# One core, cross attention: the first activations on one queue, normalised before the transpose, and later loads at other slots

## The chip, the cores and the metric

The kernel runs on one core of one Trainium2 chip. The metric is the device time of one execution in microseconds (us). The engines are named as the profile names them: PE is the matrix engine (PEld its weight loads), DVE the vector engine, ACT the scalar engine, POOL the general-purpose engine, and SP the engine that issues nearly all DMAs here. An engine works through its own instructions in order; it waits for another only on a semaphore.

## The reference

```python
x = (hidden_states - mu) * jax.lax.rsqrt(var + LN_EPS) * ln_gamma + ln_beta
Q = _split_heads(x @ Wq.T)
K = _split_heads(memory_keys)          # memory_keys and memory_values are the same ctx
V = _split_heads(memory_values)
scores = jnp.einsum('bhsd,bhtd->bhst', Q, K) * scale
scores = jnp.where(attention_mask[:, None, None, :], scores, -jnp.inf)
probs = jax.nn.softmax(scores, axis=-1)
attn = jnp.einsum('bhst,bhtd->bhsd', probs, V)
out = attn.transpose(0, 2, 1, 3).reshape(B, S, HIDDEN) @ Wout.T
return residual + out
```

There are 8 batches of 256 query rows and 256 context rows, 1024 columns, 32 heads of 32, all in float32. The mask has a batch's 256 context positions.

## The kernel before

**Slots.** The work is cut into 64 slots: slot `n` belongs to batch `n // 8` and to four heads. In each slot PE makes the scores of the next slot (`sc`), the product of probabilities and values of the slot two before (`pv`), and pieces of the query projection (`pq`, weights `wq`) and the output projection (`po`, weights `wo`). DVE adds the mask and finds the extreme of each row (`e`, `mn`), ACT takes the exponentials, POOL (and in places ACT and DVE) divides by the sum, DVE transposes blocks of 32 into `pT`, ACT puts half of that aside in `pc`, and two pairs of DMAs (`pT<-pT`, then `pT<-pc`) bring the blocks to the partitions where `pv` reads them.

**Batches.** Batches 0 and 1 take plain projections. From batch 2 on (`SPLIT = 2`) the query projection is made of seven half-size products with sums and differences of weights, and the same is done for the output projection. The derived query weights `T1` and `T3` don't fit beside the others: they are built once in a buffer called `ring`, stored to memory (`kept_T`), and loaded back into `ring` for each later batch in the order T1, B11, T3. The derived output weights are made on POOL by `sum_wo` from the loaded blocks `B11`, `B12`, `B21`, `B22`, each loaded in two pairs of chunks by `load_wo`.

**Order.** Nothing reorders the work: each engine's instructions stand as the code emits them. The tables `loads`, `stats`, `norms`, `trans`, `moves`, `rings` say at which slot a batch's `x` is loaded, normalised, transposed, and moved, and at which slot `ring` is refilled. What stands in the list `between` of a slot is issued on SP between that softmax's `pT<-pT` and its `pT<-pc`; the first eight softmaxes do this one slot later than the others. Eight DMA semaphores go round, so a DMA also waits for the eighth one before it.

**The start.** `x[0]` is loaded in two row blocks `s` = 0 and 1, 128 rows each. Block 0 comes in two column halves, one issued by SP and one by ACT; block 1 comes whole. PE first runs 26 transposes of a constant (`busy`) until data is there. For block 0, DVE subtracts the mean and builds a diagonal matrix of the reciprocal deviations, and PE multiplies each chunk by it: transposing and scaling in one product. Block 1 is normalised whole on DVE and transposed plainly. ACT and DVE copy the eight transposed chunks from `px` to `xnT` with gamma and beta (`copy_x0`), and `first_q` multiplies each chunk with the first query weights as it comes.

```python
x0 = xs[0][:, 0, :]
nc.vector.tensor_scalar(x0, x0, mean, None, ALU.subtract)
diag = ring[:, 0, 1, :]
nc.vector.tensor_scalar(diag, ident, rstds[0][:, 0:1], None, ALU.mult)
ln_stats(0, 1)
transpose_x0(0, diag)
early, late = (0, 1, 2, 3, 6, 7), (4, 5)
for c in early + late:
    copy_x0(0, c, nc.vector if c > 5 else nc.scalar)
ln_norm(0, 1, nc.vector)
first_q(0, early + late)
transpose_x0(1)
```

Of the kernel before, what the change touches and what calls it, by code (L numbers as in the profile page):

```python
# [51 lines left out]
P = 128  # L52
# [7 lines left out]
def xattn_kernel(  # L60
# [54 lines left out]


    busy = ps_s.tile([P, P], F32, tag="sc", name="busy")
    for _ in range(26):
        nc.tensor.transpose(busy, ident, ident)


    xs, ks, vs, rs = {}, {}, {}, {}

    def load_x(b, s, h=None, queue=nc.sync):
# [4 lines left out]
        queue.dma_start(xs[b][:, s, cols], x[b, ts(s, P), cols])  # L129

    def load_k(n):

# [91 lines left out]
    def ln_stats(b, s, parts=range(3), later=None):  # L224


        if s == 0 and 0 in parts:
            mvs[b] = sm.tile([P, NS, 2], F32, tag="mv", name=f"mv_{b}", bufs=2)
            rstds[b] = sm.tile([P, NS], F32, tag="rstd", name=f"rstd_{b}", bufs=2)
        if 0 in parts:  # L230
            sts[b, s] = sm.tile([P, 2, 6], F32, tag="st", name=f"st_{b}_{s}", bufs=2)
        for h in range(2):
            if h in parts:
                nc.vector.bn_stats(sts[b, s][:, h, :], xs[b][:, s, ts(h, 512)])  # L234
        if 2 not in parts:
            return
        nc.vector.bn_aggr(mvs[b][:, s, :], sts[b, s].rearrange("p h k -> p (h k)"))
        ve = sm.tile([P, 1], F32, tag="ve", name=f"ve_{b}_{s}", bufs=2)
        nc.vector.tensor_scalar(ve, mvs[b][:, s, 1:2], LN_EPS, None, ALU.add)

        def pow_():
            nc.gpsimd.tensor_tensor(rstds[b][:, s : s + 1], ve, mhalf[:, :1], ALU.pow)

        if later is None:
            pow_()
        else:
            later.append(pow_)

    def ln_norm(b, s, engine):
        if engine is nc.scalar:  # L250
            shift = sm.tile([P, 1], F32, tag="shift", name=f"shift_{b}_{s}", bufs=2)
            nc.gpsimd.tensor_scalar(
                shift, mvs[b][:, s, 0:1], rstds[b][:, s : s + 1], -1.0, ALU.mult, ALU.mult
            )
            engine.activation(
                xs[b][:, s, :], xs[b][:, s, :], AF.Identity,
                bias=shift, scale=rstds[b][:, s : s + 1],
            )
            return
        engine.tensor_scalar(  # L260
            xs[b][:, s, :], xs[b][:, s, :], mvs[b][:, s, 0:1], rstds[b][:, s : s + 1],
            ALU.subtract, ALU.mult,
        )

# [1 line left out]
    xnTs[0] = lambda c: xnT0[:, c, :]  # L266
    px0 = {}

    def transpose_x0(s, diag=None):

        pool, tag, k = (ps_v, "pv", NC // 2) if diag is None else (ps_s, "sc", 2)
        for g in range(NC // k):
            pt = pool.tile([P, k, P], F32, tag=tag, name=f"px0_{s}_{g}")
            for i in range(k):
                px0[s, k * g + i] = pt[:, i, :]
                chunk = xs[0][:, s, ts(k * g + i, P)]
                if diag is None:
                    nc.tensor.transpose(pt[:, i, :], chunk, ident)
                else:
                    nc.tensor.matmul(pt[:, i, :], chunk, diag, start=True, stop=True)  # L280

    def copy_x0(s, c, engine):

# [523 lines left out]
    for n in range(N):  # L807
# [9 lines left out]
    assert not any(n in products and new_qs[n] for n in range(N))  # L817


    loads, stats, norms, trans, moves, biases, masks = (  # L820
        {n: [] for n in range(N)} for _ in range(7)
    )
    for b in range(1, B):
        first = NQ * (b - 1) + 2
        if b == 1:
            when = dict(moves=())
        elif b == 2:
            when = dict(
                loads=(0, 1), stats=(2, 3), norms=(3, 4), trans=(4, 5),
                moves=tuple(5 + (i + 2) // 6 for i in range(16)),  # L830
            )
        else:
            when = dict(
                loads=(first - 12, first - 11) if b == SPLIT + 1 else (first - 13, first - 12),
                stats=(first - 10, first - 8) if b == SPLIT + 1 else (first - 11, first - 9),
                norms=(first - 8, first - 7), trans=(first - 7, first - 6),
                moves=tuple(first - 6 + (i + 2) // 6 for i in range(16)),
            )
        for table, key in (
            (loads, "loads"), (stats, "stats"), (norms, "norms"), (trans, "trans"),  # L840
        ):
            for i, n in enumerate(when.get(key, ())):
                assert n < first
                table[n].append((b, i))
# [42 lines left out]
    x0 = xs[0][:, 0, :]  # L887
    mean = mvs[0][:, 0, 0:1]
    nc.vector.tensor_scalar(x0, x0, mean, None, ALU.subtract)
    diag = ring[:, 0, 1, :]  # L890
    nc.vector.tensor_scalar(diag, ident, rstds[0][:, 0:1], None, ALU.mult)
# [52 lines left out]
    for n in range(N):  # L944
# [8 lines left out]
        if n + 3 in firsts or n + 2 in firsts:  # L953
            between, ahead = between + ahead, []
        if b >= 0:
            if b == B - 2 and i - 1 in (5, 6):
# [217 lines left out]
```

## Time and profile before

| | before |
|---|---|
| median of three runs | 562.32 us (562.32 to 562.91) |
| the profiled execution | 562.78 us |
| its span in the trace | 560.9 us |
| PE busy | 555.3 us, 99% of the span |
| DVE, ACT, POOL busy | 466.5 us (83%), 423.6 us (76%), 392.9 us (70%) |
| DMA queue of SP | 117.48 MB, 69.9% of sixteen engines' span |
| granted PE clock | full in all forty slices |

The span runs from the first to the last instruction on the core; the profiled execution took 1.88 us more than its span and 0.46 us more than the median run. A row of the timeline gives the start, the length, the engine, the line, what is written from what, the shapes and the count; in square brackets stands how long the engine idled before and who released it. A row with a count over one merges neighbours.

### The profile page before, as it was taken

The numbers are of one execution on the slowest core, as the hardware profiler recorded it, in microseconds if no ns is written. First come the engines' busy times: TensorE is split into PE (matmuls) and PEld (weight loads), VectorE is DVE, ScalarE is ACT, GpSimd is POOL, SyncE is SP. The second block draws the span as 40 slices with busy tenths as digits, with TensorE's granted clock in tenths as the row PEclk, the third lists the DMA queues.
The fourth block names the chain that finished last, engine by engine and source line by source line (L and its number), as shares of the span: only waits on it lengthen the run. The fifth ranks groups of instructions, "written<-read, shape, count | busy, mean of one in ns | idle before, by whom it ended". The sixth has DMA issues, their size and how long they took to land.

```text
span 560.9 us, 24340 instructions
## 1 busy us (share of the span) xinstructions
PE 555.3 (99%) x9334; PEld 356.9 (64%) x9334; DVE 466.5 (83%) x1716; ACT 423.6 (76%) x1464; POOL 392.9 (70%) x635
## 2 busy tenths in 40 slices
PE   8999999999999999999999999999999999999997
PEld 7666665767656767567765676567766766744443
DVE  5979889999998888988898888988888878879823
ACT  3699999998769867797777967778776876769920
POOL 1688887999797566867568566777648657448780
PEclk9999999999999999999999999999999999999999
DMA  8967658966688867887788677788658974536752
GB/s 301 398 189 210 184 152 239 300 191 185 203 291 244 234 186 199 271 226 235 199 244 246 197 194 220 235 236 242 180 157 242 256 214 132 145 95 182 217 161 76
DMA packets 47236, 119.30 MB, mean 213 GB/s; under 512 B 8976, under 2 KB 9744, under 8 KB 47120
## 3 DMA queue, kind: packets, MB, share of 16 engines
q1 hardware_dynamic: 46832, 117.48, 69.9%
q8 instruction: 74, 1.21, 0.9%
q14 instruction: 42, 0.34, 0.2%
q10 hardware_dynamic: 288, 0.27, 0.1%
HBM read 66.33 MB, written 11.53 MB: 139 GB/s over the span
## 4 chain that ended last, share of the span: by engine, by line
PE 97%; DVE 1%; DMA 1%; ACT 0%; POOL 0%; issue 0%; POOLq 0%
PE po_S L216 20%; PE pq_A L216 19%; PE pv L643 12%; PE sc L493 12%; PE po_A L216 11%; PE pq L216 10%; PE pq_S L216 7%; PE po_end L216 3%; PE po_last L216 1%; DMA x<-in_x_dram 1%; PE po_end_s L216 0%; PE px L280 0%; PE px L314 0%; ACT e L535 0%; DVE st L234 0%; DVE xnT L289 0%
## 5 line engine op out<-in xcount | busy, mean ns | idle before, releaser
L550 POOL TENSOR_SCALAR e<-e,rden 128x256 f32<-128x256 f32 x466 | 215.4, 479 | 124.6 <-DVE rden L542 122.1
L535 ACT ACTIVATE e<-e,mn 128x256 f32<-128x256 f32 x512 | 254.1, 502 | 43.3 <-DVE mn L531 42.8
L556 DVE STREAM_TRANSPOSE pT<-e 128x512 f32<-128x512 f32 x256 | 178.9, 703 | 36.6 <-POOL e L550 27.7
L531 DVE CUSTOM_DVE_ANT_0 e<-sc,mb 128x256 f32<-128x256 f32 x512 | 185.3, 416 | 23.5 <-PE sc L493 23.1
L562 ACT COPY pc<-pT 128x512 f32<-128x512 f32 x128 | 78.9, 616 | 53.1 <-DVE pT L556 34.7
L535 ACT ACTIVATION_READ_ACCUMULATOR e<-e,mn 128x1 f32 x512 | 98.4, 192 | 0.0
L493 PEld LDWEIGHTS sc<-k,qa 32*128 32x128 f32 x1024 | 46.1, 184 | 45.7 <-issue 20.8
L643 PE MATMUL pv<-pT,v 64*32 64x128 f32 x4096 | 74.5, 274 | 0.0
L493 PE MATMUL sc<-k,qa 32*128 32x256 f32 x1024 | 73.7, 401 | 0.2 <-ACT qa L301 0.2
L216 PE MATMUL po_S<-wo,at 128*64 128x512 f32 x304 | 73.5, 599 | 0.0
L643 PEld LDWEIGHTS pv<-pT,v 64*32 64x32 f32 x4096 | 57.2, 105 | 22.8 <-issue 10.8
L216 PE MATMUL po_A<-wo,at 128*64 128x512 f32 x256 | 58.6, 599 | 0.0
L216 PE MATMUL pq<-xnT,wq 128*64 128x256 f32 (+3 forms) x544 | 58.4, 369 | 0.0
L216 PEld LDWEIGHTS pq_A<-xnT,wq 128*64 128x64 f32 x832 | 46.3, 137 | 7.4 <-issue 6.3
L216 PE MATMUL po_S<-wo,s 128*64 128x512 f32 x208 | 49.5, 599 | 0.0
L216 PEld LDWEIGHTS pq<-xnT,wq 128*64 128x64 f32 x544 | 36.8, 137 | 18.8 <-issue 1.8
L216 PE MATMUL pq_A<-xnT,wq 128*64 128x128 f32 x832 | 47.6, 273 | 0.0
L542 DVE RECIPROCAL rden<-den 128x2 f32<-128x2 f32 x256 | 38.3, 150 | 5.9 <-ACT e L535 4.9
L531 DVE DVE_READ_ACCUMULATOR2_ANT mn<- 128x1 f32 x512 | 42.5, 83 | 0.0
L216 PEld LDWEIGHTS po_A<-wo,at 128*64 128x64 f32 x256 | 16.9, 137 | 30.0 <-issue 29.1
L216 PEld LDWEIGHTS po_S<-wo,at 128*64 128x64 f32 x304 | 19.3, 137 | 22.6 <-issue 22.6
L656 ACT COPY at<-pv 128x128 f32<-128x128 f32 x128 | 26.1, 253 | 8.7 <-PE pv L643 8.7
(99 smaller groups left out, 645.2 us busy)
## 6 DMA issues: line engine op xcount, KB each, us to landing
v<-in_kv_dram SPq DMA_DIRECT2D x32, 512.0 KB, 4.6
pT<-pT SPq DMA_DIRECT2D x128, 128.0 KB, 2.8
pT<-pc SPq DMA_DIRECT2D x128, 128.0 KB, 4.1
ring<-kept_T SPq DMA_DIRECT2D x20, 512.0 KB, 6.0
k<-in_kv_dram SPq DMA_DIRECT2D x32, 256.0 KB, 4.3
x<-in_x_dram SPq DMA_DIRECT2D x15, 512.0 KB, 6.0
r<-in_x_dram SPq DMA_DIRECT2D x28, 256.0 KB, 5.0
out_dram<-r SPq DMA_DIRECT2D x28, 256.0 KB, 2.8
```

The source lines that it names most:

```text
L216: nc.tensor.matmul(out[ts(w, P // 2)], stationary[:, ts(w, P // 2)], moving, **flags)
L493: nc.tensor.matmul(scs[n][j][:, s, :], qa[r, n % NQ, ts(s, P)], ks[n - n % 2][r, n % 2, :], start=True, stop=True,)
L531: nc.vector.tensor_tensor_reduce(out=e[:, s, :], in0=pss[j][:, s, :], in1=mbs[n // NQ], scale=1.0, scalar=NO_SCORE, op0=ALU.add, op1=ALU.m ...
L535: nc.scalar.activation(e[:, s, :], e[:, s, :], AF.Exp, bias=mn[:, s : s + 1], scale=-1.0, accum_out=den[:, s : s + 1],)
L542: nc.vector.reciprocal(rden, dens[j])
L550: engine.tensor_scalar(es[j][:, s, :], es[j][:, s, :], rden[:, s : s + 1], 1.0, ALU.mult, ALU.mult,)
L556: nc.vector.transpose(pT[:, :, :, j, :, :].rearrange("p a i s k -> p (a i) s k"), es[j].rearrange("p s (b t) -> p b s t", t=K),)
L562: nc.scalar.copy(pc[:, :, ts(j, 2)], pT[:, 1, :, ts(j, 2)])
L643: nc.tensor.matmul(pvs[n][r][j * HD : (j + 1) * HD], vs[n - n % 2][ts(r, 2 * K), i, ds(n % 2 * P + j * HD, HD)], pT[ts(r, 2 * K), :, i, j, ...
L656: nc.scalar.copy(ats[b, k][:, c, :, ts(r, 2), :], pv.rearrange("p a s k -> p s a k"))
```

## The change

The start and four groups of later loads are different; the counts of PE's, POOL's and ACT's instructions after the start, and their order, are the same.

- All of `x[0]` goes on SP, in four halves; ACT issues no load of `x`.
- DVE normalises block 0 in two halves with both operands at once (`ln_norm` gained a parameter `h`), and PE transposes it plainly. The statistics of block 1's first half stand ahead of that, those of its second half behind it.
- ACT copies five of the eight chunks and DVE three (it was six and two), and the products take them in another order. Block 1 is normalised in halves too. `busy` has 25 transposes.
- `x[2]`'s block 0 is loaded in the prologue and its block 1 in slot 0; two loads of output weights move from the prologue to slots 1 and 2, and two from slots 2 and 4 to slots 3 and 5.
- `T1` for batch 3 is loaded into `ring` in slots 14 and 15 (it was 15 and 16); `x[4]` is loaded at the end of slot 12 and in slot 13 (it was 13 and 14).

```diff
-    for _ in range(26):
+    for _ in range(25):
         nc.tensor.transpose(busy, ident, ident)
...
     load_x(0, 0, 0)
-    load_x(0, 0, 1, nc.scalar)
+    load_x(0, 0, 1)
     nc.scalar.activation(gs[:, :NS], mhalf, AF.Exp)
     nc.scalar.dma_start(gb, gamma_beta)
-    load_x(0, 1)
+    load_x(0, 1, 0)
+    load_x(0, 1, 1)
...
-    for which, pair in ((B12, 0), (B22, 0), (B11, 0), (B12, 1), (B22, 1), (B11, 1)):
+    for which, pair in ((B12, 0), (B22, 0), (B11, 0), (B12, 1)):
         load_wo(which, pair)
...
-                loads=(0, 1), stats=(2, 3), norms=(3, 4), trans=(4, 5),
+                loads=(-1, 0), stats=(2, 3), norms=(3, 4), trans=(4, 5),
...
+        if b == SPLIT + 2:
+            loads[first - 13], loads[first - 12] = [(b, 1)], []
+            at_end[first - 14].append((b, 0))
...
-        for slots, name in (((n - 3, n - 2), "T1"), ((n, n), "B11"), ((n + 2, n + 2), "T3")):
+        soon = n - 4 if b == SPLIT + 1 else n - 3
+        for slots, name in (((soon, soon + 1), "T1"), ((n, n), "B11"), ((n + 2, n + 2), "T3")):
...
     ln_stats(0, 0)
...
-    ln_stats(0, 1)
-    transpose_x0(0, diag)
-    early, late = (0, 1, 2, 3, 6, 7), (4, 5)
-    for c in early + late:
-        copy_x0(0, c, nc.vector if c > 5 else nc.scalar)
+    ln_stats(0, 1, (0,))
+    for h in range(2):
+        ln_norm(0, 0, nc.vector, h)
+    transpose_x0(0)
+    ln_stats(0, 1, (1, 2))
+    arrive = (0, 1, 2, 3, 5, 4, 6, 7)
+    for c in arrive:
+        copy_x0(0, c, nc.vector if c > 4 else nc.scalar)
     nc.gpsimd.tensor_copy(xnT0[:, :, S], bet)
-    ln_norm(0, 1, nc.vector)
-    first_q(0, early + late)
+    for h in range(2):
+        ln_norm(0, 1, nc.vector, h)
+    first_q(0, arrive)
...
+    load_x(SPLIT, 0)
...
-        if n in (2, 4):
-            between.append(partial(load_wo, B21, n // 2 - 1))
+        for which, pair in {1: ((B22, 1),), 2: ((B11, 1),), 3: ((B21, 0),), 5: ((B21, 1),)}.get(n, ()):
+            between.append(partial(load_wo, which, pair))
...
+        for args in at_end[n]:
+            load_x(*args)
```

DVE's first instructions before; the line is the code's, `st`, `mv`, `ve`, `rstd` are the statistics of a row, and the tile of `x[0]` is `x_150`:

```order
L234 BN_STATS st_0_184<-x_150 128x6 x2
L237 BN_AGGR mv_182<-st_0_184 128x2
L239 TENSOR_SCALAR ve_0_188<-mv_182 128x1
L889 TENSOR_SCALAR x_150<-x_150,mv_182 128x1024
L891 TENSOR_SCALAR ring<-ring,rstd_183 128x128
L234 BN_STATS st_1_193<-x_150 128x6 x2
L237 BN_AGGR mv_182<-st_1_193 128x2
L239 TENSOR_SCALAR ve_1_197<-mv_182 128x1
L289 TENSOR_SCALAR xnT_181<-px_0_3_209,gb 128x128 x2
L260 TENSOR_SCALAR x_150<-x_150,mv_182,rstd_183 128x1024
```

The same place after, with `x[0]` in `x_149`:

```order
L235 BN_STATS st_0_182<-x_149 128x6 x2
L238 BN_AGGR mv_180<-st_0_182 128x2
L240 TENSOR_SCALAR ve_0_186<-mv_180 128x1
L235 BN_STATS st_1_189<-x_149 128x6
L262 TENSOR_SCALAR x_149<-x_149,mv_180,rstd_181 128x512 x2
L235 BN_STATS st_1_189<-x_149 128x6
L238 BN_AGGR mv_180<-st_1_189 128x2
L240 TENSOR_SCALAR ve_1_207<-mv_180 128x1
L287 TENSOR_SCALAR xnT_179<-px_0_2_199,gb 128x128
L287 TENSOR_SCALAR xnT_179<-px_0_3_202,gb 128x128 x2
L262 TENSOR_SCALAR x_149<-x_149,mv_180,rstd_181 128x512 x2
```

The subtraction and the diagonal are gone, two half normalisations stand in their place with half of block 1's statistics on either side, and a third copy has come to DVE.

SP's queue around slots 12 to 14 before; `x_2402` is `x[4]`, the pairs `pT` and `pc` are those of softmaxes 14 and 15, `kept_T_148` holds T3, and `kept_T_146`, further on, T1:

```order
L339 DMA xnT_2251<-xe_2091 32x512 x4
L621 DMA pT_2343<-pT_2343 32x1024 x2
L143 DMA v_2400<-in_kv_dram 128x1024
L129 DMA x_2402<-in_x_dram 128x1024
L625 DMA pT_2343<-pc_2344 32x1024 x2
L339 DMA xnT_2251<-xe_2091 32x512 x6
L409 DMA kept_T_148<-ring 128x1024
L770 DMA out_dram<-r_1_0_2082 128x512
L621 DMA pT_2500<-pT_2500 32x1024 x2
L135 DMA k_2560<-in_kv_dram 128x512
L129 DMA x_2402<-in_x_dram 128x1024
L625 DMA pT_2500<-pc_2501 32x1024 x2
```

The same place after; `x_2257` is `x[4]`, and `kept_T_145` holds T1:

```order
L337 DMA xnT_2252<-xe_2092 32x512 x4
L129 DMA x_2257<-in_x_dram 128x1024
L619 DMA pT_2346<-pT_2346 32x1024 x2
L143 DMA v_2403<-in_kv_dram 128x1024
L129 DMA x_2257<-in_x_dram 128x1024
L623 DMA pT_2346<-pc_2347 32x1024 x2
L337 DMA xnT_2252<-xe_2092 32x512 x6
L407 DMA kept_T_147<-ring 128x1024
L768 DMA out_dram<-r_1_0_2083 128x512
L619 DMA pT_2502<-pT_2502 32x1024 x2
L135 DMA k_2562<-in_kv_dram 128x512
L417 DMA ring<-kept_T_145 128x1024
```

Block 0 of `x[4]` now stands ahead of softmax 14's pairs, block 1 takes the place that block 0 had, and the first half of T1 the place of block 1. The second half of T1 stands where the first half stood, and its old place one softmax later (not shown) is empty.

SP's queue around slots 4 and 5 after; `xnT_1171` is the transposed `x[2]`, and the pairs are those of softmaxes 6 and 7:

```order
L619 DMA pT_1109<-pT_1109 32x1024 x2
L143 DMA v_1272<-in_kv_dram 128x1024
L172 DMA wo<-in_woT_dram 128x2x512
L623 DMA pT_1109<-pc_1110 32x1024 x2
L337 DMA xnT_1171<-xe_1026 32x512 x6
L619 DMA pT_1259<-pT_1259 32x1024 x2
```

The row of `wo` is new in this group; before it stood one softmax earlier, with softmax 5's pairs.

More of the change, by code (lines that the diff above doesn't have):

```diff
@@ L117, in xattn_kernel, with load_x @@
     busy = ps_s.tile([P, P], F32, tag="sc", name="busy")
-    for _ in range(26):
+    for _ in range(25):
         nc.tensor.transpose(busy, ident, ident)
     xs, ks, vs, rs = {}, {}, {}, {}
-    def load_x(b, s, h=None, queue=nc.sync):
+    def load_x(b, s, h=None):
         if b not in xs:
@@ L128, in load_x @@
         cols = ds(0, D) if h is None else ts(h, 512)
-        queue.dma_start(xs[b][:, s, cols], x[b, ts(s, P), cols])
+        nc.sync.dma_start(xs[b][:, s, cols], x[b, ts(s, P), cols])
     def load_k(n):
@@ L247, in ln_stats, with ln_norm @@
             later.append(pow_)
-    def ln_norm(b, s, engine):
+    def ln_norm(b, s, engine, h=None):
+        cols = ds(0, D) if h is None else ts(h, 512)
         if engine is nc.scalar:
@@ L255, in ln_norm @@
             engine.activation(
-                xs[b][:, s, :], xs[b][:, s, :], AF.Identity,
+                xs[b][:, s, cols], xs[b][:, s, cols], AF.Identity,
                 bias=shift, scale=rstds[b][:, s : s + 1],
@@ L260, in ln_norm @@
         engine.tensor_scalar(
-            xs[b][:, s, :], xs[b][:, s, :], mvs[b][:, s, 0:1], rstds[b][:, s : s + 1],
+            xs[b][:, s, cols], xs[b][:, s, cols], mvs[b][:, s, 0:1], rstds[b][:, s : s + 1],
             ALU.subtract, ALU.mult,
@@ L267, in xattn_kernel, with transpose_x0 @@
     px0 = {}
-    def transpose_x0(s, diag=None):
-        pool, tag, k = (ps_v, "pv", NC // 2) if diag is None else (ps_s, "sc", 2)
+    def transpose_x0(s):
+        pool, tag, k = (ps_s, "sc", 2) if s == 0 else (ps_v, "pv", NC // 2)
         for g in range(NC // k):
@@ L275, in transpose_x0 @@
                 px0[s, k * g + i] = pt[:, i, :]
[L276 to L280, printed above, removed]
+                nc.tensor.transpose(pt[:, i, :], xs[0][:, s, ts(k * g + i, P)], ident)
     def copy_x0(s, c, engine):
@@ L817, in xattn_kernel @@
     assert not any(n in products and new_qs[n] for n in range(N))
-    loads, stats, norms, trans, moves, biases, masks = (
-        {n: [] for n in range(N)} for _ in range(7)
+    loads, stats, norms, trans, moves, biases, masks, at_end = (
+        {n: [] for n in range(N)} for _ in range(8)
     )
@@ L843, in xattn_kernel @@
                 assert n < first
-                table[n].append((b, i))
+                if n >= 0:
+                    table[n].append((b, i))
+        if b == SPLIT + 2:
+            loads[first - 13], loads[first - 12] = [(b, 1)], []
+            at_end[first - 14].append((b, 0))
         for n in range(N):
@@ L952, in xattn_kernel @@
         ahead = rings[n]
-        if n + 3 in firsts or n + 2 in firsts:
+        if n + 3 in firsts or n + 2 in firsts or firsts.get(n + 4) == SPLIT + 1:
             between, ahead = between + ahead, []
```

5 lines of the change are left out of this document (removed).

## The prediction

> **What bounds the kernel now.** I read the page first, then PE's waits over the whole span, then the chain at the start, then the timeline there. Of the page, the span, the engines and the shares of the chain:
>
> ```profile
> span 560.9 us, 24340 instructions
> PE 555.3 (99%) x9334; PEld 356.9 (64%) x9334; DVE 466.5 (83%) x1716; ACT 423.6 (76%) x1464; POOL 392.9 (70%) x635
> PE 97%; DVE 1%; DMA 1%; ACT 0%; POOL 0%; issue 0%; POOLq 0%
> ```
>
> PE is busy for 99% of the span and is 97% of the chain. All its waits, with total, count and longest:
>
> ```profile
> PE busy L119 <- POOL ring masks.py:199: 1.3, 1, 1.3
> PE px L280 <- DVE ring L891: 1.2, 1, 1.2
> PE sc L493 <- ACT qa L301: 0.2, 1, 0.2
> ```
>
> After 16.2 us PE never waits visibly. So a change can gain in two ways only: start PE's real work earlier, or give it less to do. It can lose wherever a transfer or another engine comes late for PE. The chain up to the transposes of block 1 (start, length, what):
>
> ```profile
> 0.72 3.68 DMA x<-in_x_dram
> 4.43 1.30 DVE st L234 x2
> 5.75 0.22 DVE mv L237
> 6.00 0.16 DVE ve L239
> 6.30 0.93 POOL rstd L242
> 7.26 0.30 DVE ring L891
> 7.60 2.05 PE px L280 x16
> 9.65 1.90 PE pq L216 x32
> 11.55 1.04 PE px L278 x8
> ```
>
> The load takes until 4.40, two statistics until 5.73, the power on POOL lies at 6.30, and PE begins at 7.60. From there to 11.5 PE alone is the chain: 2.05 us of products with the diagonal, then 1.90 us of projection. The other engines in that stretch, and SP's first two issues:
>
> ```profile
> 0.72 0.86 SPq L129 DMA_DIRECT2D x<-in_x_dram  x2
> 7.46 1.28 DVE L234 BATCH_NORM_STATS2 st<-x 128x6 f32<-128x512 f32 x2
> 8.35 2.21 ACT L287 ACTIVATE xnT<-px,gb 128x128 f32<-128x128 f32 x6 [5.69 <-PE px L280]
> 9.25 0.55 POOL L242 TENSOR_TENSOR rstd<-ve,mhalf 128x1 f32<-128x1 f32 x1 [2.03 <-DVE ve L239]
> 9.69 0.73 DVE L289 TENSOR_SCALAR xnT<-px,gb 128x128 f32<-128x128 f32 x2 [0.52 <-PE px L280]
> 10.34 0.81 DVE L260 TENSOR_SCALAR x<-x,mv,rstd 128x1024 f32<-128x1024 f32 x1
> 11.48 1.09 PE L278 MATMUL px<-ring,x 128*128 128x128 f32 x8
> ```
>
> **The change, step by step. The load.** What was landed when, by the issues in windows at the start (KB, us to landing):
>
> ```profile
> x<-in_x_dram SPq DMA_DIRECT2D x1, 256.0 KB, 3.7
> x<-in_x_dram SPq DMA_DIRECT2D x1, 512.0 KB, 4.6
> ```
>
> Before, the two halves of block 0 left together, and SP's was in at 4.4. Block 1, issued at about 1.15 (half of 0.86 behind 0.72), was in at 5.75. So its 512 KB took 1.35 us behind the halves, 0.67 per 256 KB. With one queue the first half need not share: I put it 0.45 us earlier, at 3.95 (an estimate, below the 0.67 because the first bytes are late whatever follows). The second half lands at 4.4 if only bytes count, at 4.83 if its issue, 0.43 later, counts in full; I take 4.6, nearer the bytes, since each landing waits 3.7 us on an issue of 0.43. Statistics of 0.64 each then run from 3.95 and from 4.6, and end at 5.24 instead of 5.71: **0.47 gained**, with bounds 0.2 (second half at 4.83) and 0.64 (both in by then, one statistic wholly hidden).
>
> The Trainium skill ("DMA: Bandwidth & Descriptors", "Issuing engines are not separate DMA queues") says that queues of different engines share the same 16 DMA engines, and a second issuer saves only the issue time. By that rule alone the second half would be 0.43 late and the gain 0.2 to 0.25, so the sum would be 561.6 in place of 561.4; no run here shows which.
>
> **To PE's start.** From the statistics' end to PE's start stand mv, ve, rstd and the diagonal. The diagonal's 0.30 becomes a half normalisation: a whole one took 0.81, so 0.45 with the fixed part of a small operation (estimate; 0.40 to 0.5). The subtraction of 1024 columns vanishes, but it stood beside POOL's 0.93 and cost nothing. Half of block 1's statistics, 0.64, takes its place under the same cover, if its half of the load has landed by 5.7, about when the whole was in before. Net **0.15 lost**: PE starts at about 7.3, 0.3 earlier.
>
> **Transposes, copies, projection.** Sixteen instructions of 0.128 become eight; the plain transposes of block 1 took 1.09 for eight. PE would save 0.96, but now ACT's copies are what PE waits for. First copy before: 0.75 behind PE's start; now one pair fewer, 0.25 less, so at 7.3 + 0.5 = 7.8. The six copies took 2.21, some 0.35 apart, the last one 0.46 long. The fourth chunk (c = 3) is out at 7.8 + 3 x 0.35 + 0.46 = 9.31, and ACT's fifth (c = 4) at 9.66. DVE's second half normalised is done by 7.65, block 1's second statistic with mv and ve costs 1.05, so its copies (0.73 for two) start at about 8.7 and are out at 9.1, 9.45 and 9.8: in time. PE takes 1.90/8 = 0.24 a chunk: from 9.31 five chunks to 10.5, where before block 1's transposes began at 11.48. **In all 0.95 gained** at that point: 0.3 from the earlier start, 0.65 of the 0.96.
>
> **Behind it.** Block 1's power (0.55 on POOL, ready by 9.4) and its halves on DVE (from 9.8, first out at 10.25) are there before 10.5. The last visible wait, 0.2 on ACT, stays. One transpose less in `busy` lies in the idle time before PE's start and is worth nothing; if data came before it ended, it would save 0.1.
>
> **Moved loads.** PE waits for none now, so moving them gains nothing itself; the question is whether they find PE 0.95 earlier still in time. The tightest places, each as PE's row, SP's issue, and landing:
>
> ```profile
> 37.47 0.81 PE L643 MATMUL pv<-pT,v 64*32 64x128 f32 x39
> 33.68 1.14 SPq L625 DMA_DIRECT2D pT<-pc  x2
> pT<-pc SPq DMA_DIRECT2D x2, 128.0 KB, 2.3
> 89.99 1.16 PE L643 MATMUL pv<-pT,v 64*32 64x128 f32 x64
> 83.90 1.15 SPq L625 DMA_DIRECT2D pT<-pc  x2
> 165.37 1.16 PE L643 MATMUL pv<-pT,v 64*32 64x128 f32 x64
> 159.35 1.74 SPq L625 DMA_DIRECT2D pT<-pc  x2
> pT<-pc SPq DMA_DIRECT2D x2, 128.0 KB, 4.7
> 167.36 2.90 PE L216 MATMUL pq_S<-sx,ring 128*64 128x128 f32 x50
> 163.64 0.44 SPq L419 DMA_DIRECT2D ring<-kept_T  x1
> ring<-kept_T SPq DMA_DIRECT2D x20, 512.0 KB, 6.0
> 62.84 2.53 POOL L182 TENSOR_TENSOR wo<-wo 128x512 f32<-128x512 f32 x2
> ```
>
> - The first `pv` at 37.47: the second pair issue at 34.3 lands 2.3 later, at 36.6, with 0.9 to spare. It is held by the prologue's loads, not by PE, so it would not move along by itself. The prologue now carries five loads behind the query weights and not six: 512 KB less, 0.67 x 2 = 1.3 earlier. Cover stays. Without it, PE would lose about 0.1.
> - At 89.99, landing at about 84.5 + 4.7 = 89.2, 0.8 to spare. In this stretch SP issues without pause, and a weight load now stands one softmax ahead of it: 0.45 of SP's time (the size of the other issues), perhaps 1.3 of transfer. The chain in front hangs on PE and the vector engines and moves along; I expect 0.3 to spare.
> - At 165.37, landing near 165.1 (159.35, the second up to 1.1 later, 4.7 behind): 0.3 to 0.5 to spare. The number of loads ahead of it is the same. If SP's queue moves along with the start, it holds.
> - The half of T1 issued at 163.64 lands by the median at 169.6, and the product wants its second half at 167.36 + 1.75 = 169.1: no room at all. A slot earlier it has some eight.
> - The output weights of slots 1 to 5 land long before POOL's first use of one of them at 62.84; the one moved into slot 1 is issued some 20 us ahead.
>
> All places together: 0. Bounds: 0.1 gained (small hidden waits) and 0.95 lost.
>
> **Sum.** 560.9 - 0.47 + 0.15 - 0.65, rounded: 559.95, so 562.78 - 0.95 = 561.83 for the profiled execution. That execution stood 0.46 over the median of 562.32; against the median it is **561.4**, 0.17% less.
>
> **Rivals.**
> - *Slower: the weight load in slot 5 stops SP.* SP's queue waits for the eighth DMA before; the sixth of the moves behind that load waits for the load itself, and behind that move stands the first pair for the `pv` at 89.99. That pair's issue, and the output weights' median landing:
>
> ```profile
> 79.91 1.16 SPq L621 DMA_DIRECT2D pT<-pT  x2
> wo<-in_woT_dram SPq DMA_DIRECT2D x8, 512.0 KB, 10.5
> ```
>
> Landing 10.5 behind an issue at about 72, it would hold SP until 82.5. From the pair's issue to the last landing is 89.2 - 79.9 = 9.3, so 91.8, where PE, 0.95 earlier, wants it at 89.0: 2.8 lost, 561.4 + 2.8 = 564.2. The whole gain is lost if SP is held past 80.7, a landing 8.7 behind the issue. Against it: six of the eight loads behind that median left in the full queue of the prologue, and over the span the queue is 70% used. Chance 0.07.
> - *Slower: a cold clock.* The warm-up rows, whole and for the first nineteen:
>
> ```profile
> 1.34 5.06 PE L119 MATMUL busy<-ring 128*128 128x128 f32 x26 [1.34 <-POOL ring masks.py:199]
> 1.34 4.30 PE L119 MATMUL busy<-ring 128*128 128x128 f32 x19 [1.34 <-POOL ring masks.py:199]
> ```
>
> Nineteen transposes take 4.30, 0.226 each, the last seven 0.76, 0.109 each: PE doubles its pace after some 4 us. If plain transposes did not hold that pace, the projection behind them would run at half speed, 1.90 more: 563.3. But `busy` is transposes alone and reached the pace. Chance 0.03. The Trainium skill ("TensorE: Matmul & The Clock Gate", "Part 4: PE-mode transpose") says that transposes don't raise the clock; the trace disagrees.
> - *The gain goes at a later place.* Any of the three tight `pv`, with its transfer not moving along, takes back up to 0.95: 561.8 to 562.3. Chance 0.17.
> - *The load gains more*, first half in by 3.75 and second by 4.3: 0.35 more, and a hidden wait gone: 561.0. Chance 0.23.
>
> **How the numbers follow.** The likeliest, 0.50, is 561.4, its own range 561.1 to 561.8. What a measurement of this kernel can tell from no change is 0.2%, 1.1 us: 561.2. Faster takes most of the larger gain, 0.19, and a quarter of the likeliest, 0.13: 0.32. Slower is the first two rivals, 0.10. The rest, 0.58, is the same. The range goes from 560.7 (0.64 and 0.96 both in full) to 562.6, leaving out the two slow rivals and the ends.
>
> **What would show it.** After: the first statistic at about 4.0; one half normalisation ending near 7.3; eight transposes of `px` in about 0.95 and PE's first row of `pq` waiting a little on ACT; block 1's transposes at 10.5; PE's busy time down by some 0.9. A new row among PE's waits, from `pT` or `ring`, would show the third rival; a second statistic that starts over 4.8 would show the load wrong. If several moved loads relieve waits that PE's rows hide, I am wrong on the fast side.

## The result, and the profile after

The changed kernel takes 566.16 us (median of six runs, 564.75 to 566.94), the kernel before beside it 562.61 (562.32 to 562.91): a ratio of 1.0056, with a 95% interval of 1.0041 to 1.0071. It is 0.56% slower; forecast was 561.4, in a range of 560.7 to 562.6. The profiled execution took 565.37 us, of it 563.0 in the span, so 2.37 outside it where the kernel before has 1.88. From here on "span" is a kernel's median span over its runs, where nothing else is said: 564.0 for the changed kernel. Two of the twelve runs of the kernel "wo and x[2] back" were in a slower state and don't count in its row.

The page's lines on the span, PE and the chain:

```profile
span 563.0 us, 24323 instructions
PE 555.9 (99%) x9325; PEld 356.6 (63%) x9325; DVE 467.0 (83%) x1718; ACT 423.5 (75%) x1463; POOL 392.4 (70%) x635
PE 78%; DMA 6%; ACT 5%; POOL 4%; DVE 3%; issue 2%; SPq 1%; POOLq 0%; DVEq 0%; ACTq 0%
```

PE's share of its span still reads 99%. The chain tells more: PE had 97% of it, now 78%. Its waits (engine, line, releaser: total, count, longest):

```profile
PE busy L119 <- POOL ring masks.py:199: 1.3, 1, 1.3
PE pv L641 <- ACT pc L560: 0.9, 1, 0.9
PE px L278 <- DVE x L262: 0.6, 1, 0.6
PE pv L641 <- ACT qa L359: 0.6, 1, 0.6
PE pq L217 <- DMA wq<-in_wq_dram: 0.4, 1, 0.4
PE po_S L217 <- DVE r L767: 0.2, 1, 0.2
PE sc L491 <- ACT qa L299: 0.2, 1, 0.2
```

Four of the seven are new. The start (timeline rows of DVE and PE, SP's first issues, and the landing of the first query weights):

```profile
0.72 1.81 SPq L129 DMA_DIRECT2D x<-in_x_dram  x4
2.58 0.43 SPq L166 DMA_DIRECT2D wq<-in_wq_dram  x1
wq<-in_wq_dram SPq DMA_DIRECT2D x1, 512.0 KB, 6.2
3.69 0.69 DVE L235 BATCH_NORM_STATS2 st<-x 128x6 f32<-128x512 f32 x1 [3.69 <-DMA x<-in_x_dram]
4.97 0.69 DVE L235 BATCH_NORM_STATS2 st<-x 128x6 f32<-128x512 f32 x1 [0.58 <-DMA x<-in_x_dram]
7.44 1.11 PE L278 MATMUL px<-ring,x 128*128 128x128 f32 x8 [0.61 <-DVE x L262]
8.91 1.97 PE L217 MATMUL pq<-xnT,wq 128*64 128x128 f32 x32 [0.35 <-DMA wq<-in_wq_dram]
10.81 1.09 PE L278 MATMUL px<-ring,x 128*128 128x128 f32 x8
```

Block 1's transposes begin 0.67 earlier than before (11.48), not 0.95. The last wait ahead of the projection is for the query weights: issued at 2.58 instead of 1.63, since two more issues of 0.45 stand ahead of them, and in at 8.8 (2.58 + 6.2).

The lead of 0.67 is gone at 82.5. SP's issues there, its wait, the landing of the first `pT<-pc` pair below, and PE's rows from there to 167:

```profile
73.60 0.45 SPq L172 DMA_DIRECT2D wo<-in_woT_dram  x1
74.15 1.16 SPq L623 DMA_DIRECT2D pT<-pc  x2
75.36 7.26 SPq L337 DMA_DIRECT2D xnT<-xe  x6
82.73 1.17 SPq L619 DMA_DIRECT2D pT<-pT  x2
SPq L337 <- DMA wo<-in_woT_dram: 2.6, 1, 2.6
pT<-pc SPq DMA_DIRECT2D x2, 128.0 KB, 7.9
82.51 1.25 PE L641 MATMUL pv<-pT,v 64*32 64x128 f32 x64 [0.60 <-ACT qa L359]
91.41 1.08 PE L217 MATMUL po_A<-wo,at 128*64 128x512 f32 x4
104.51 1.94 PE L217 MATMUL po_S<-wo,s 128*64 128x512 f32 x8 [0.20 <-DVE r L767]
167.17 1.45 PE L641 MATMUL pv<-pT,v 64*32 64x128 f32 x64 [0.87 <-ACT pc L560]
```

The weight load of slot 5 leaves at 73.60; the pair of `pT` behind it lands 7.9 after its issue, by 82.6, so the wait is probably a DMA's though the row names ACT. The sixth move waits 2.6 for that load; it leaves at about 82.1 (75.36 + 7.26, less the 0.5 of its own issue), 8.5 behind the load's issue, and the next `pT<-pT` leaves at 82.73 instead of 79.91. Before, the same rows of PE began at 82.49, 91.07, 103.80 and 165.37: a lead of 0.67 has become a lag of 0.71 at 104 and of 1.80 at 167. The chain shows both stretches:

```profile
88.98 7.04 DMA x<-in_x_dram
96.03 2.29 DMA xnT<-xe
98.71 1.29 POOL sx L440
...
102.48 1.26 POOL r L758
103.76 0.70 DVE r L767
104.51 1.50 PE po_S L217 x5
...
150.44 6.00 DMA ring<-kept_T
156.45 2.60 DMA xnT<-xe
159.38 1.29 POOL sx L440
...
162.03 3.64 POOL e L548 x8
165.70 0.72 DVE pT L554
166.44 0.63 ACT pc L560
167.17 1.45 PE pv L641 x63
```

In the first, SP's late queue issues `x[3]` at 88.98, a move (`xnT<-xe`) follows its landing, and POOL's sums wait behind that. In the second, half of T1, at its new slot, is in the chain itself.

### The profile page after: what moved, and what is told of

Read it like the earlier page. It is cut to its first block, busy times and chain, and to the rows that moved or that the text cites. A ratio compares the mean times of both kernels' runs of the same rounds, so it can differ in the third digit from the quotient of the medians.

```text
span 563.0 us, 24323 instructions
## 1 busy us (share of the span) xinstructions
PE 555.9 (99%) x9325; PEld 356.6 (63%) x9325; DVE 467.0 (83%) x1718; ACT 423.5 (75%) x1463; POOL 392.4 (70%) x635
## 4 chain that ended last, share of the span: by engine, by line
PE 78%; DMA 6%; ACT 5%; POOL 4%; DVE 3%; issue 2%; SPq 1%; POOLq 0%; DVEq 0%; ACTq 0%
PE po_S L217 20%; PE pq_A L217 18%; PE pv L641 10%; PE sc L491 10%; PE po_A L217 8%; PE pq_S L217 7%; ACT e L533 3%; PE po_end L217 3%; POOL e L548 2%; DMA xnT<-xe 2%; DMA x<-in_x_dram 1%; PE po_last L217 1%; DMA pT<-pT 1%; DMA wq<-in_wq_dram 1%; DMA ring<-kept_T 1%
```

## The experiments

Each kernel was timed beside the kernel before on the same chip. "PE at" gives the start of PE's rows in one trace: block 1's transposes, the output product at 103.80 and the `pv` at 165.37 of before; "SP held" is SP's wait for output weights between 70 and 92.

| kernel | ratio to before (95%) | span, before's beside it | outside | PE at | SP held |
|---|---|---|---|---|---|
| changed | 1.0056 (1.0041 to 1.0071) | 564.0 | 2.19 | 10.81, 104.51, 167.17 | 2.6 |
| start alone | 1.0030 (1.0010 to 1.0049) | 562.5, 561.3 | 2.13 | 10.76, 103.44, 165.30 | 0 |
| start alone, again | 1.0037 (1.0019 to 1.0055) | 562.5, 561.1 | 2.12 | 10.61, 104.57, 166.28 | 0 |
| loads alone | 1.0030 (1.0013 to 1.0048) | 562.2, 561.3 | 1.84 | 11.36, 104.55, 166.26 | 1.7 |
| wo and x[2] back | 1.0041 (1.0012 to 1.0071) | 563.2, 561.3 | 2.18 | 10.60, 103.50, 165.40 | 0.3 |
| T1 and x[4] back | 1.0065 (1.0036 to 1.0094) | 563.6, 561.3 | 2.17 | 10.62, 102.97, 166.02 | 1.4 |
| pair in slot 4 | 1.0044 (1.0029 to 1.0060) | 562.6, 561.2 | 2.18 | 10.68, 103.08, 165.26 | 0 |
| nine more products | 1.0061 (1.0032 to 1.0090) | 564.2, 561.2 | 2.19 | 10.74, 103.45, 166.05 | 1.7 |
| x[3] early | 1.0044 (1.0017 to 1.0071) | 562.2, 561.2 | 2.15 | 10.79, 104.81, 167.79 | 0.5 |
| wq0 on ACT | 1.0079 (1.0053 to 1.0105) | 564.9, 561.2 | 2.12 | 11.31, 104.14, 165.78 | 0 |
| before, again | 1.0002 (0.9989 to 1.0016) | 561.2, 561.4 | 1.76 | 11.48, 103.79, 165.29 | 0 |
| late start | 1.0014 (1.0003 to 1.0025) | 561.5, 561.4 | 2.15 | 11.19, 103.50, 165.00 | 0 |
| pair 4, T1 and x[4] back | 1.0035 (1.0014 to 1.0057) | 563.0, 561.4 | 2.20 | 10.12, 102.45, 164.32 | 0 |
| queue only | 1.0002 (0.9991 to 1.0013) | 561.3, 561.4 | 1.76 | 10.81, 103.15, 164.87 | 0 |
| changed, late start | 1.0015 (1.0004 to 1.0026) | 561.9, 561.3 | 2.19 | 11.72, 104.09, 165.93 | 0 |
| two more on DVE | 1.0010 (0.9998 to 1.0021) | 561.0, 561.3 | 2.13 | 11.36, 103.71, 165.25 | 0 |
| old start, wo moved | 1.0019 (1.0000 to 1.0038) | 561.0, 561.3 | 1.86 | 11.33, 105.99, 167.63 | 2.6 |
| pair 4, no T1 | 1.0014 (0.9999 to 1.0030) | 561.9, 561.3 | 2.20 | 10.52, 102.88, 164.43 | 0 |
| late, block 1 whole | 0.9995 (0.9982 to 1.0007) | 561.1, 561.4 | 1.86 | 11.23, 104.32, 165.92 | 0 |

A trace is one execution; the spans of one kernel lie 2 to 7 us apart, so times are judged by ratios, places by traces. A traced run can be far from its kernel's median: that of "pair 4, T1 and x[4] back" is the slowest of twelve (span 566.0), that of "pair 4, no T1" the fastest (559.6). The ratio is not the quotient of two medians either: for "loads alone" the medians, 564.04 and 563.18, give 1.0015 where the table has 1.0030.

### Which part: start or loads

**Start alone:** the kernel before with the new start; no load behind it moved.

```diff
-        for which, pair in {1: ((B22, 1),), 2: ((B11, 1),), 3: ((B21, 0),), 5: ((B21, 1),)}.get(n, ()):
+        for which, pair in {2: ((B21, 0),), 4: ((B21, 1),)}.get(n, ()):
```

> The kernel before with the new start alone; all later loads stand where they stood. The changed kernel's trace shows the start 0.67 us earlier at block 1's transposes, then new waits of PE: 0.9 and some tenths near 82 to 90, 0.4 near 100, 1.2 near 165. Theory A (loads): these waits come from the moved loads, so here they are absent and the gain stays: 562.6 - 0.67 = 561.9, range 561.6 to 562.3. Theory C (start): the rest of the kernel can't follow an earlier PE, SP's queue above all, and the waits come from that: pT for the products near 90 and 165 late again, 562.6 to 565.

Neither theory as told. No wait for weights, so the one at 82 is the loads'. But the lead of 0.72 still shrinks to 0.36 at 103 and 0.07 at 165, without help from a moved load; at 88 DVE waits for `x[3]`:

```profile
DVE st L235 <- DMA x<-in_x_dram: 0.4, 1, 0.4
```

And the time is worse, not better, by 0.30%.

**Loads alone:** the old start, with `loads=(-1, 0)`, `at_end`, `soon` and the slots 1, 2, 3 and 5 of the change.

> The kernel before with its own start; the four groups of later loads are moved as in the changed kernel. Theory A: the waits stand near 82, 90 and 165 at nearly their full size, since PE is only 0.67 later and the loads are late by their own queue: 562.6 + 2.8 - up to 1.3 (two places relieved by 0.67) = 564.1 to 565.4. Theory C: nothing is late with the old start: 562.4 to 562.9.

Theory A in kind: SP is held 1.7, `po_S` begins at 104.55. The time, 564.04, is just under its range. The loads cost even where PE has no lead, 0.30% together by the ratio.

**Output weights and x[2] back** in the changed kernel (`loads=(0, 1)`, six pairs in the prologue, slots 2 and 4).

> The changed kernel with the output weights and the two blocks of x[2] loaded as before; T1 and x[4] stay at the new slots. Theory A1 (only the output weights in slots 3 and 5 do harm): the waits near 82 and 90 are gone and the one near 165 with them, since SP recovered: 561.9. Theory A2 (T1 and x[4] do harm by themselves near 140 to 167, 1.4): 562.6 - 0.7 + 1.4 = 563.3. The waits near 82 to 100 (1.4 in the changed kernel) are absent by both.

The waits at 82 to 91 are gone, as expected; the lead of 0.88 falls to 0.30 at 103 and to nothing at 165, which fits neither number. In this trace PE starts early, and it shows what the products then wait for:

```profile
6.78 1.11 PE L278 MATMUL px<-ring,x 128*128 128x128 f32 x8 [0.69 <-DVE x L262]
8.70 1.97 PE L217 MATMUL pq<-xnT,wq 128*64 128x128 f32 x32 [0.81 <-DMA wq<-in_wq_dram]
```

**T1 and x[4] back** in the changed kernel:

```diff
-        soon = n - 4 if b == SPLIT + 1 else n - 3
+        soon = n - 3
...
-        if b == SPLIT + 2:
-            loads[first - 13], loads[first - 12] = [(b, 1)], []
-            at_end[first - 14].append((b, 0))
```

> The changed kernel with T1 for batch 3 and x[4] loaded at the slots of before; output weights and x[2] stay moved. Theory A1: the waits near 82 to 100 stay, 1.4: 562.6 - 0.7 + 1.4 = 563.3, and more if 165 stays late. Theory A2 alone (output weights harmless): 561.9. Both: 563.3 with nothing late near 140 to 167.

Both expectations miss: SP is held 1.4 and PE doesn't feel it in this run; 1.3 is lost at 165 with T1 at its old slots. So moving T1 isn't needed for a loss there.

### Single causes

**The second pair of B21 in slot 4**, all else as changed: `3: ((B21, 0),), 4: ((B21, 1),)`.

> The changed kernel with the second pair of weights B21 loaded in slot 4 instead of slot 5; everything else as changed. In the changed kernel SP waits 2.6 for that load at 82.1, and the pairs pT for the products at 82.5 and 90.1 land with nothing to spare. Theory A1 (this one load does it): SP's wait of 2.6 on the weights is gone, the product at 82.5 starts 0.6 to 0.7 earlier, the one at 91.4 as well, and the projection piece that starts at 104.5 in the changed kernel starts at 103.4 to 103.6, as in the kernel with the new start alone. Span 1.0 lower, 562.0. Theory D (the queue is full there whatever its order): another load is waited for, and that piece starts at 104.2 or later; span 562.7 or more.

Theory A1, by the trace: SP waits for no weights, and PE keeps its lead (0.72 at 103) up to 165, where `pT` is late. The span, 562.6, misses the 562.0 of A1 and nearly reaches the 562.7 of D.

```profile
165.26 1.45 PE L641 MATMUL pv<-pT,v 64*32 64x128 f32 x64 [0.62 <-DMA pT<-pc]
```

That span is 1.6 lower than that of the next kernel, which has the pair in slot 5 (same set); their ratios' intervals overlap, so the size is uncertain.

**Nine more products** behind the changed kernel's last one (`for _ in range(9): nc.tensor.matmul(tail, ...)`).

> The changed kernel with nine more small products on PE behind its last one, which nothing reads: as many products as the kernel before has. In kernels with the new start an execution takes 2.1 us more than its span and at times 3.3, in those with the old start 1.8; the traces show PE's last fetch of instructions behind the end of the span in two of the former and at 555 in the kernel before. Theory F (the length of PE's instructions sets where that last fetch falls): 1.8 again, and the median execution 0.3 to 0.5 under the changed kernel's with the same span, 563 to 564. Theory G (the start itself lies outside the span, by its first transfers): 2.1 as before, no difference.

Theory F falls for the median, 2.19 outside as in the changed kernel, and fits the outliers: none of the eight runs of this kernel has over 2.27 outside, while kernels with the changed kernel's count of products have single runs of 2.4 to 5.6.

**x[3] early:** start alone with `loads=(first - 13, first - 12)` for batch 3.

> The kernel with the new start and the old later loads, with x[3] loaded one slot earlier, in slots 5 and 6. There DVE waits 0.4 for x[3] at 88.2, and PE's lead over the kernel before falls from 0.72 to 0.36 at 103 and 0.07 at 141. Theory H (the landing of x[3] holds DVE, and DVE has no slack up to 141): DVE's wait is gone, the lead stays 0.6 to 0.7 at 103 and 141, and is lost at 165 at the earliest; span 561.0 to 561.4. Theory D (the queue is full there): another transfer is late by as much, pT above all, and the lead at 103 is 0.4 or less; span 561.4 or more.

Theory D: DVE no longer waits there, but SP's moves now wait 2.5 for a load of `x`, and `po_S` begins at 104.81. In that stretch, in this trace, an earlier load is paid by another. Two `pv` wait for `pT` later, at 167.79 and 541.07.

```profile
SPq L337 <- DMA x<-in_x_dram: 2.5, 1, 2.5
```

**wq0 on ACT:** start alone, with `nc.scalar.dma_start(wq[:, 0], wq_[0])` behind gamma and beta.

> The kernel with the new start and the old later loads, with the first query weights issued by ACT behind gamma and beta instead of by SP as its fifth load. With SP they are issued at 2.58 and in at 8.5 to 8.8, and in no run do the products begin before 8.6, though the transposes began at 6.8 in one. Theory S (those weights set the start of the products): issued about 1.1 earlier, they are in by 7.9 to 8.2, the products begin at 8.2 to 8.4 (the copies' time), block 1's transposes at 10.1 to 10.3. Rival (the transfers share 16 engines, and order counts for nothing): in at 8.5 or later, block 1's transposes at 10.6 to 10.8; or x[0] is late in turn, and PE starts its transposes after 7.4.

The rival: the weights come ahead of block 1 of `x[0]`, for which DVE, in the new order, waits before it normalises block 0. PE's transposes begin at 8.03:

```profile
6.84 0.69 DVE L235 BATCH_NORM_STATS2 st<-x 128x6 f32<-128x512 f32 x1 [1.02 <-DMA x<-in_x_dram]
8.03 1.11 PE L278 MATMUL px<-ring,x 128*128 128x128 f32 x8 [2.41 <-DVE x L262]
```

The loss of this run lies elsewhere, though. Its PE is 0.1 behind the kernel before at 292 (`po_A` at 292.60, before 292.50) and 2.8 behind at 429 (429.34, before 426.55). Its only waits between are three of "issue", time in which PE waited for nothing that the profile shows:

```profile
331.91 0.44 PE L217 MATMUL pq_A<-sx,wq 128*64 128x128 f32 x4 [0.64 <-issue]
383.81 0.55 PE L217 MATMUL pq_S<-xnT,wq 128*64 128x128 f32 x6 [0.84 <-issue]
```

The third is 0.32 at 346.07. What they are is open; this kernel has all its later loads where they were.

### The lead, T1, and the queue

**Before, again**, for a trace from this chip.

> The kernel before, unchanged, on the chip of the experiments, for a trace to lay beside theirs. If its trace is like the first one (no wait of PE between 16 and 540, the product at 165.4 in time), what the other kernels lose at 165 is theirs: 562.5 to 563. If it loses 0.3 or more there as well, that loss is the chip's and not the change's.

In time at 165 (165.29); its trace loses 0.4 near 300. The loss at 165 is not the chip's.

**Late start:** start alone, `for _ in range(41)` instead of 25.

> The kernel with the new start and the old later loads, with 41 transposes of a constant at the start instead of 25, 16 x 0.109 = 1.7 more, so that PE's real work begins as late as in the kernel before or a little later (transposes of x[0] at 8.1, block 1's at 11.4 to 11.5). Theory C (PE's lead is what makes transfers and vector work late): no lead, and no waits behind 16: span that of the kernel before within 0.2, its runs as close together (560.5 to 562), and with 0.3 more outside the span 563.2 against 563.0. Theory K (something else in the start's code costs, on DVE or in the queue): waits near 100 and 165 as in the kernel with the new start alone, span 561.9 to 563, runs as far apart as there.

Theory C fits: block 1's transposes begin 0.4 later than with the start alone, a lead of 0.29 is left, it stays whole past 165 (165.00), and the span is back within 0.2 of before's. Of the 0.48 between the medians of the times, 0.35 lie outside the span.

**Pair in slot 4, T1 and x[4] back**, the two edits above together.

> The changed kernel with the second pair of weights B21 in slot 4 and with T1 for batch 3 and x[4] at the slots of before. With the pair in slot 4 alone PE kept its lead of 0.80 up to 165 and lost 1.0 there. Theory A2 (T1 and x[4] at the new slots cause that loss): the lead stays past 165, span 560.3 and 562.5 in all, level with the kernel before. Theory C (the stretch from 140 to 167 doesn't follow an earlier PE, with either order): 0.8 or more is lost at 165 as well, span 561.2 to 561.6.

Theory C, though this run is the slowest of its kernel. The weights came early here (5.2 behind their issue, not 6.2), the lead was 1.36, `pv` was nearly in time, and then the second half of T1 stopped PE, the place the prediction called without room:

```profile
wq<-in_wq_dram SPq DMA_DIRECT2D x1, 512.0 KB, 5.2
10.12 1.09 PE L278 MATMUL px<-ring,x 128*128 128x128 f32 x8
169.28 1.97 PE L217 MATMUL pq_S<-sx,ring 128*64 128x128 f32 x32 [0.88 <-DMA ring<-kept_T]
```

**Queue only:** the kernel before, with `x[0]` in four halves on SP and nothing else.

> The kernel before with only its first loads changed: all of x[0] on SP in four halves; VectorE's work, the products and all other loads as before. My step for the load put a first half at 3.95 and a second at 4.6 and a gain of 0.47. Theory L (queue): the halves land at 3.5 and 4.3 to 5.0, the first query weights at 8.5 to 8.8 instead of 7.84, which hides nothing here because the products begin at 9.2 or later: PE 0.3 to 0.5 earlier at block 1's transposes, lost again by 165; 562.8 to 563.5, and the time outside the span tells whether the queue (2.1) or VectorE's work (1.8) adds the 0.3 seen there. Rival (the statistics wait for the second half as long as they did): block 1's transposes at 11.4 or later.

Sixteen products with the diagonal and the whole old work of DVE, and block 1's transposes begin at 10.81, as in the changed kernel:

```profile
6.95 2.04 PE L281 MATMUL px<-ring,x 128*128 128x128 f32 x16
8.91 1.97 PE L217 MATMUL pq<-xnT,wq 128*64 128x128 f32 x32
10.81 1.09 PE L279 MATMUL px<-ring,x 128*128 128x128 f32 x8
```

So nearly all of the start's gain is the queue's: with the whole new start and its 25 transposes, the traces in which the first half of `x[0]`'s block 0 was followed at once by the second have 10.52 to 10.79 there, and one, in which the weights came a microsecond sooner, 10.12. Outside the span stand 1.76: the queue isn't what adds 0.35. The time is level.

### The account

**Changed kernel, late start:** 41 transposes instead of 25.

> The changed kernel with 41 transposes of a constant at the start instead of 25, so that PE's real work begins about as late as in the kernel before; all loads at the new slots. Theory C (PE's lead is what makes them late): the loss nearly vanishes, median span 561.3 to 562.0, with 0.35 more outside it 563.5 to 564.2. Theory A (the moved loads cost by themselves, above all the pair in slot 5): median span 562.2 or more, as with the old start and the moved loads, 564.4 or more in all.

Theory C: 1.0015 against 1.0056. A cost of 0.6 of span is left; the rest goes with the later start, or with the 16 more transposes, which this run doesn't separate.

**Two more instructions on DVE**, behind all work of the kernel before (`for _ in range(2): nc.vector.tensor_copy(tail, mhalf)`).

> The kernel before with two more small copies on VectorE behind its last work, which nothing reads. By the traces VectorE has 2101 to 2102 instructions in all kernels that take 1.8 us outside their span and 2103 to 2104 in all that take 2.1. Theory F (the number of its instructions sets it, as instructions are fetched in blocks): 2.1. Theory G (something in the work of the new start sets it): 1.8. The span as before, 561.2 to 561.5, by both.

Theory F: 2.13 outside (2.06 to 2.23 in ten runs), where the kernel before never has over 1.92.

**Old start, output weights and x[2] moved**, T1 and `x[4]` as before.

> The kernel before with its own start, where only the output weights and x[2] are loaded as in the changed kernel, the second pair of B21 in slot 5; T1 and x[4] as before. With all loads moved, the old start lost 0.9 in the median span. Theory A1 (the pair in slot 5 does it): 0.6 to 0.9 here as well, median span 562.0 to 562.3, SP waiting up to 2.6 for the weights near 82 and the product at 91 late. Theory A2 (T1 and x[4]): as before, 561.2 to 561.6.

Both, run by run: seven of twelve spans lie at 560.6 to 561.2, five at 562.6 to 567.0. The median is before's, the ratio just above 1. The traced one (563.3) is one of the five, and shows the mechanism without any lead of PE:

```profile
SPq L340 <- DMA wo<-in_woT_dram: 2.6, 1, 2.6
```

**Pair in slot 4, no T1 for batch 3:** `if b > SPLIT and (b, name) != (SPLIT + 1, "T1"):`.

> The changed kernel with the second pair of B21 in slot 4, and with the load of T1 for batch 3 left out (two transfers of 512 KB, in slots 14 and 15; the product that reads it takes what stands in the buffer). With the pair in slot 4 alone PE led by 0.80 up to 165 and lost 1.0 there, where pT landed at 165.46. Theory D (the transfers of that stretch take the lead back): pT lands before 164.3, the lead stays 0.6 to 0.8 past 171; median span 1.0 under that kernel's 562.6, 561.5 or less. Rival (vector work sets that stretch): the product at 165.3 as late as there, lead gone, 562.3 to 562.9.

Theory D in the trace, which is of the kernel's fastest run: `pv` and the product behind it keep a lead of 0.94, and PE waits for nothing behind the start (span of that run 559.6).

```profile
164.43 1.16 PE L641 MATMUL pv<-pT,v 64*32 64x128 f32 x64
166.42 3.66 PE L217 MATMUL pq_S<-sx,ring 128*64 128x128 f32 x64
```

The median span, 561.9, is lower than with T1 (562.6), but misses 561.5 and is still 0.6 over before's, so T1 is not the whole of the loss.

**Late start, block 1 whole:** one DVE instruction fewer (`ln_norm(0, 1, nc.vector)`).

> The kernel with the new start, the old later loads and 41 transposes of a constant, in which VectorE normalises block 1 of x[0] in one piece, one instruction fewer: 2102 by the traces' count. Theory F: 1.8 outside the span instead of 2.15. With the late start's median span of 561.5 that makes 563.3 against 563.2 for the kernel before, no difference. If 2.1 stays outside, the limit lies lower or it is not this number; then 563.6.

1.86 outside, and level with before. With the later start and one DVE instruction fewer, nothing of the loss is left.

**Start alone, again.**

> The kernel with the new start and the old later loads, a second time. If PE's lead costs by itself even with the old loads (theory C in full): ratio 1.002 to 1.004 again, median span 1.0 over that of the kernel before. If the lead is only taken back, as with the first loads alone, the time outside the span (0.35) is all that is lost: ratio 1.0000 to 1.0012, median span within 0.4 of the kernel before.

It costs by itself: 1.0037. This trace shows a second chain that isn't the queue. Between 59.9 and 166.2 the chain that ended last has no piece of PE in it: POOL has 55 us of it, DVE 28, ACT 7, and transfers 7 (two `pT<-pT`). The work of POOL and DVE is as long there as PE's, and a PE that starts earlier meets it.

What stays open is why the median run loses more than its lead. An early PE is neither enough nor needed: the queue alone has it at 10.81 and is level, and "wq0 on ACT" starts block 1's transposes at 11.31, later than the late start's 11.19, and has the highest ratio of all. One rival stands untested. With the old later loads, all four kernels that lose (start alone twice, x[3] early, wq0 on ACT) have 9325 of PE's products, and all that are level have 9334 or 9341; the 16 transposes that delay PE also move every later instruction of PE back in its order. A run that adds such instructions without a delay would tell the two apart. No version here beats the kernel before by more than can be measured.

## Why the prediction was wrong

- **The load.** Mis-sized. In the profiled run the first statistic starts at 3.69 (forecast 3.95), the second at 4.97 (4.6, and over the 4.8 named as the sign of error), so statistics end 0.05 earlier, not 0.47. The sum by the Trainium skill's rule ("DMA: Bandwidth & Descriptors", "Issuing engines are not separate DMA queues"), 0.2 to 0.25, was nearer in this run. But this run is not typical: in 11 of the 15 traces with four halves on SP the second statistic follows the first at once, and both end at 4.85 to 5.11, 0.6 to 0.9 earlier than before. There the rival "the load gains more" was right, and both sums were too small. (The upper bound of 0.64 didn't follow from its own terms: with the first half in at 3.95, two statistics of 0.64 end at 5.23 at the earliest.)
- **Transposes, copies, projection.** The step failed in its bound. I took ACT's copies as the last to arrive; it is the first query weights, for which the sum has no term, though two issues were put ahead of them. In the run where PE began at 6.78 the products still began at 8.70. Hence 10.81, not 10.5; and halving the transposes and the normalisation bought at most 0.3 over the queue alone.
- **The cold clock** didn't happen: eight transposes take 1.11, and the products behind them 1.97, as long as the same timeline row before (at 9.58).
- **Moved loads, "All places together: 0", with 0.95 as the most that could be lost.** This is the step that failed most. The bound says that at worst the lead is lost. The start alone, with no load moved, lost its lead and 1.2 to 1.4 of span besides; the loads alone, with no lead, 0.8. In the profiled run the largest piece is the rival with the weight load in slot 5, which got 0.07: the trace shows SP's release at 82.1 (I wrote 82.5). I weighed it by its landing of 10.5 from a full prologue and dismissed it by an average, 70% use of the queue; it landed 8.5 behind its issue. Its first victim was not the one I named but `pT` issued next to it, as late as the load. From 0.67 ahead to 0.71 behind, 1.4 are lost by 104, and not 2.8. It is one cause of several: with the pair in slot 4 this wait is gone and the ratio is still 1.0044.
- **"Moves along".** I wrote that the chain in front of 89.99 "hangs on PE and the vector engines and moves along", and of 165 "if SP's queue moves along with the start, it holds". Neither moves along. Start alone, again, has POOL and DVE as the chain up to 166. At 165 the `pT` is late with T1 at the new slots; with the old ones T1 itself is, or `pT` in another run. A lead of over 0.5 passes in one trace alone, that without T1's transfers; the late start's 0.29 passes with them.
- **Not in the sum at all:** 0.3 to 0.4 outside the span.

From the runs: 0.4 of the loss lie outside the span; delaying PE (with 16 more transposes) gives 2.1 of span back; 0.6 of span are left then: 3.1 of the 3.55. The rest is not assigned.

## What to carry to other kernels

A kernel that is 99% bound by one engine can have a second chain just as long, here the work of POOL and DVE and SP's queue with its transfers: before you forecast an earlier start, ask of each tight place what it hangs on, and if the answer is not the engine that starts earlier, count the lead as lost there. The waits of the engine don't show that chain beforehand: PE had no visible wait behind 16.2 us. Judge the room of a moved load by the queue in that slot (what waits for the eighth DMA before, which small pair lands behind it), not by the average use of the span. And when an issue is put ahead of others on a queue, look at what stands behind it: here the first query weights, which seemed to have room, came to hold the products.

## What the runs showed of the hardware

- Two more instructions on DVE, behind all its work, added 0.34 us outside the span (1.79 to 2.13). Kernels with 1716 or 1717 instructions of DVE on the page have 1.76 to 1.86 outside, those with 1718 have 2.12 to 2.20, whatever else differs. Why, no run shows.
- Fewer products on PE go with outliers: of 97 runs of kernels with 9325 of PE's products on the page, 27 took over 2.4 us outside the span, of 93 with 9334 or more none (the most is 2.28). In the spans of the former the page counts 73 packets of the instruction queue, in those of the latter 74.
- A weight load of 512 KB landed 8.5 after its issue, and two `pT` transfers of 128 KB issued just behind it 7.9, where 2.3 was seen at 33.68 in the kernel before: these small transfers landed about when the large one ahead of them did.
